# FFN of an MLA layer: the first low-rank input takes the place of one row of the quarter sums, VectorE adds the second one while it evacuates PSUM

## The chip, the core and the metric

The kernel runs on one core of a Trainium2 chip. The metric is the device time of one execution in microseconds (us); of several executions the median is given. The core has a matrix engine (TensorE, PE in the profile, with its weight loads shown as PEld), three engines for elementwise work (VectorE or DVE, ScalarE or ACT, GpSimd or POOL), SyncE (SP), which here only issues transfers, and 16 DMA engines. Each engine carries out its own queue of instructions in order and waits on semaphores for the others.

## The reference

The input x is 8 x 256 x 512, that is 2048 rows of 512. Each row is normalised to xn. An attention part gives s from xn (128 heads, a latent of 64, a rope part of 64), an FFN gives g, and the output is x + s * g. Only the FFN bears on this change. Its weights are quarters that are tiled four times over the inputs, each with a low-rank addition of rank 2:

```python
def _layernorm(x, axis=-1, eps=1e-05):
    m = jnp.mean(x, axis=axis, keepdims=True)
    v = jnp.var(x, axis=axis, keepdims=True)
    return (x - m) / jnp.sqrt(v + eps)
...
    def _qlora_linear(x, wq, A, B):
        w = jnp.tile(wq, (1, 4))
        base = x @ w.T
        lora = x @ A.T @ B.T
        return base + lora * LORA_SCALING
    gate = jax.nn.silu(_qlora_linear(x, w1q, a1, b1))
    up = _qlora_linear(x, w3q, a3, b3)
    return _qlora_linear(gate * up, w2q, a2, b2)
...
x = L0_attn_x
xn = _layernorm(x, axis=-1)
s = _L0_attn_ref(xn, ...)
g = _silu(_L0_ffn_ref(xn, ...))
x = x + s * g
```

w1q and w3q are 1376 x 128, w2q is 512 x 344. Because a weight is tiled four times, x @ w.T is the sum of the four quarters of a row (128 values) times the 128-row quarter weight.

## The kernel before

The program first runs the FFN over all rows (`first_phase`, L304 on), writes the gates to DRAM and then runs the attention, which reads them at its end. The order of the instructions is written out by hand: each engine's queue has the order in which the code issues the instructions, with no scheduler between. All transfers are issued on SP's queue. PSUM has eight banks of 128 x 512 values in float32, one tag for all tiles; a bank comes free when its reader is done. Pools hand out buffers in turn: `f1` has one buffer for a tag, `f2` two.

The rows go in four blocks of 512 (`tb`). The FFN of a block has these parts:

- `norm` (L371 to L403) takes the statistics of the four 128-row tiles on VectorE (L376, L377), and then the reciprocal root in three Newton steps, on VectorE in block 0 and on GpSimd in the others (L393 to L402, 14 small steps). `norm_rest` scales the tiles, on VectorE in block 0 (L412), on ScalarE else (L410).
- `turn` transposes the block on PE (16 transpositions, tile `xpt`, L420); ScalarE copies the even and VectorE the odd results to SBUF (L423, L425). Then the four quarters are added to `xs` (L429 to L431).
- `narrow` computes `pm` on PE (L172), which holds the low-rank inputs of w1 (partitions 0, 1) and w3 (partitions 32, 33), both again at 64 and 96, and the rope keys. VectorE scales it to `mid` (L446). The low-rank inputs are then rows of `mid`. `down` computes `pp` for the attention, and `sum_x` (L157) makes sums of x for the attention, four subtractions on GpSimd.
- The hidden values, 1376, are cut into 11 chunks of 128 columns (the last three hold 88 columns of three quarters, and pieces of the fourth at partitions 96 on). They go in pairs `u` = 0 to 5; the last has one chunk. For each chunk, `low` (L473) starts the banks `px` and `py` with a matmul over the two low-rank rows (two partitions contracted), and `main` adds w1 and w3 times `xs` to them (four matmuls each of 32 output columns and 512 moving ones, L172, called as a `px` or `py` group), evacuates `px` with silu on ScalarE into `gate` (L488, two buffers), and multiplies `gate` with `py` on VectorE (L490, or L493 and L494 for the last three chunks) into `hT`.
- `fold` adds up the hidden quarters on GpSimd (L508 to L510), `low_out` takes their low-rank inputs (four matmuls a third at L520; at the end VectorE adds four parts, L532), and `gate_out` multiplies with w2 (tiles `pf`) and stores the gates.

Between these parts, other work of the attention is put into the queues: `between(0)` calls `set_up` (L598 to L623), which loads `raw`, the mask and others, and rearranges them on GpSimd (L611 on); later calls stand in the last block.

At the start 48 transpositions of the identity (L552) keep PE busy while x is loaded. `load_chunks` fetches the weights in the chunk layout, for w1, w3 and four copies of b13 (the low-rank weights b1 and b3: rows 0, 1 and 32, 33 of a 34-row array). The loop that sets the order of a block is the one at the end of `first_phase`:

```python
            for u in range(6):
                low(tb, u)
                main(tb, u)
                if u in (2, 4):
                    fold(tb, u // 2 - 1)
                    low_out(tb, u // 2 - 1)
                if u == 1 and more:
                    stats = norm(tb + 1)
...
            if more:
                turn(tb + 1)
                low_out(tb, 2)
                narrow(tb + 1)
                down(tb + 1)
```

Of the kernel before, what the change touches and what calls it, by code (L numbers as in the profile page):

```python
# [9 lines left out]
F32 = mybir.dt.float32  # L10
I32 = mybir.dt.int32
AF = mybir.ActivationFunctionType
ALU = mybir.AluOpType
# [24 lines left out]
def mla_ffn_gate_kernel(  # L38
# [42 lines left out]
    cs_d = [dram.tile([P, TB], F32, name=f"cs_d{n}") for n in range(NTB)]  # L81
    krs_d = [dram.tile([R, TB], F32, name=f"kr_d{n}") for n in range(NTB)]
# [221 lines left out]
    def first_phase(between):  # L304
# [8 lines left out]
        b13_sb = fw.tile([98, NCH, P], F32, name="b13_sb")  # L313
# [4 lines left out]
        xts, xns, xnT, xsum, mids = {}, {}, {}, {}, {}  # L318
# [8 lines left out]
        def load_chunks(to, of):  # L327

            of = of.rearrange("p (q f) -> p q f", q=4)
            nc.sync.dma_start(  # L330
                out=to[:, 0:8].rearrange("p (q n) m -> p q (n m)", q=4), in_=of[:, :, 0:256]
            )
            nc.sync.dma_start(out=to[:, 8:11, 0:88], in_=of[:, 0:3, 256:344])
            nc.sync.dma_start(
                out=to[:, 8:10, 96:128],
                in_=of[:, 3, 256:320].rearrange("p (m i) -> p m i", m=2),
            )
            nc.sync.dma_start(out=to[:, 10, 96:120], in_=of[:, 3, 320:344])

        for t in (w1_sb, w3_sb, b13_sb):  # L340
            nc.gpsimd.memset(t[:, 8:11, 88:96], 0.0)
            nc.gpsimd.memset(t[:, 10, 120:128], 0.0)
# [18 lines left out]
        for n in range(2):  # L361
            for k in range(2):
                load_chunks(
                    b13_sb[64 * n + 32 * k : 64 * n + 32 * k + 2], b13[32 * k : 32 * k + 2, :]
                )
        load_chunks(w1_sb, w1t)
        load_chunks(w3_sb, w3t)
        load_x(1)

        def norm(tb):  # L370


            mv = f2.tile([P, 4, 2], F32, tag="mv", name=f"mv_{tb}")
            for n in range(4):
                s6 = f2.tile([P, 6], F32, tag="st", name=f"st_{tb}_{n}")
                nc.vector.bn_stats(s6, xts[tb][n])  # L376
                nc.vector.bn_aggr(mv[:, n, :], s6)  # L377
# [21 lines left out]
            off = f2.tile([P, 4], F32, tag="off", name=f"off_{tb}")  # L399
            if tb:  # L400
                nc.gpsimd.tensor_mul(off, mv[:, :, 0], r)
# [12 lines left out]
        def turn(tb):  # L414
            a = f1.tile([P, KT, TB], F32, tag="act1", name=f"act1_{tb}")
            xnT[tb] = a
            for n in range(4):
# [4 lines left out]
                if n % 2 == 0:  # L422
# [4 lines left out]
            xs = f2.tile([P, TB], F32, tag="xs", name=f"xs_{tb}")  # L427
# [549 lines left out]
```

## Time and profile before

The time before is 2010.74 us, the median of three runs (2010.64 to 2012.42). The profile was taken in an execution of its own:

| quantity | us |
|---|---|
| profiled execution, its own time | 2012.79 |
| its span, from the first to the last instruction of the profile | 2011.0 |
| span before the first transposition of x | 11.2 |
| from there to the first `pm` of block 1 | 42.5 |
| to that of block 2 | 51.5 |
| to that of block 3 | 48.2 |
| the last block of the FFN, with attention work in it | 85.1 |
| the attention | 1772.5 |
| VectorE busy in these four stretches of the FFN | 19.2, 19.5, 19.6, 20.2 |
| ScalarE busy in them | 13.9, 13.6, 14.0, 22.3 |
| GpSimd busy in them | 25.9, 24.4, 21.9, 49.2 |

One median `px` matmul over two low-rank rows (L473) is listed with 0.64 us, one over 128 partitions and 32 output columns (L172) with 0.59; four of the latter run side by side, and matmuls overlap, so that a group's time is read from the distance of starts and not from the sum of durations. Evacuating a bank with silu takes 0.60 (L488), the product on VectorE 0.69 (L490).

How to read the profile: the first part of its page gives each engine's busy time and share of the span. A line of the timeline gives the start, the length, engine, line of the code, operation, what is written and read with its size, and how many were merged; in square brackets the idle time before it and what ended that. The chain that ended last goes back from the last instruction, at each step to what released it or to the instruction before it on its engine. `SPq` is the queue that issues the transfers.

### The profile page before, as it was taken

To read this page: it belongs to the slowest core of one execution; us is meant where nothing else is said; L and a number is where in the kernel's file an instruction comes from. 1 tells how busy PE (TensorE), PEld (TensorE's weight loads), DVE (VectorE), ACT (ScalarE), POOL (GpSimd) and SP (SyncE) were. 2 spreads that over 40 slices of the span, in tenths; PEclk is the share of its full clock that TensorE was granted. 3 is DMA by queue.
4 is the path that set the end of the run, shared out by engine and by line. 5 is a ranking of instruction groups with operands and counts; after the bars stand their busy time and mean duration, and the time that the engine had idled before them with its cause. 6 is when DMAs were issued, how large, how long until landed. Compare 5 with 4: busy or idle time off the path is not lost.

```text
span 2011.0 us, 86602 instructions
## 1 busy us (share of the span) xinstructions
PE 1998.9 (99%) x38112; PEld 1412.7 (70%) x38112; DVE 1522.8 (76%) x2601; ACT 1079.4 (54%) x2958; POOL 725.9 (36%) x1076
## 2 busy tenths in 40 slices
PE   9999999999999999999999999999999999999998
PEld 4334577777777777777777767777777767777776
DVE  4332387878788777878787877878787877888788
ACT  2222365565556554555655645565565555556654
POOL 5445545545552323233233233223323323232231
PEclk9999999999999999999999999999999999999999
DMA  5233322222223223222223233222223222222212
GB/s 169 87 113 135 113 95 84 68 87 86 86 82 123 80 91 112 91 87 78 74 86 123 66 112 105 84 81 86 81 92 102 90 93 81 86 86 72 80 55 70
DMA packets 118188, 184.78 MB, mean 92 GB/s; under 512 B 10450, under 2 KB 84082, under 8 KB 117812
## 3 DMA queue, kind: packets, MB, share of 16 engines
q1 hardware_dynamic: 117812, 179.23, 26.4%
q8 instruction: 302, 4.95, 1.0%
q14 instruction: 74, 0.61, 0.1%
HBM read 145.12 MB, written 34.08 MB: 89 GB/s over the span
## 4 chain that ended last, share of the span: by engine, by line
PE 97%; DVE 2%; issue 0%; DMA 0%; ACT 0%; POOL 0%; SPq 0%; DVEq 0%
PE q L172 39%; PE sc L688 34%; PE av L734 11%; PE po L172 2%; PE pf L172 2%; PE px L172 2%; PE py L172 2%; PE px L473 1%; PE pm L172 1%; PE qq L250 1%; PE vps L285 1%; PE pp L172 1%; DVE pt L717 1%; DVE nmx L701 0%; PE pm L520 0%; PE xpt L420 0%
## 5 line engine op out<-in xcount | busy, mean ns | idle before, releaser
L707 ACT ACTIVATE pr<-sc,nmx 128x256 f32<-128x256 f32 x2048 | 816.5, 502 | 473.8 <-DVE nmx L701 471.0
L701 DVE TENSOR_REDUCE nmx<-sc 128x2 f32<-128x512 f32 x1024 | 635.6, 683 | 291.3 <-PE sc L688 267.4
L717 DVE STREAM_TRANSPOSE pt<-pr 128x512 f32<-128x512 f32 x1024 | 635.2, 678 | 0.0
L172 PE MATMUL q<-x,ws 128*32 128x256 f32 x8192 | 488.9, 379 | 0.6 <-POOL ws L136 0.6
L688 PE MATMUL sc<-act,qr 32*128 32x256 f32 x8192 | 489.0, 374 | 0.0
L215 POOL TENSOR_TENSOR e<-e,e 128x256 f32<-128x256 f32 x128 | 93.8, 733 | 1057.5 <-ACT e L210 570.6
L688 PEld LDWEIGHTS sc<-act,qr 32*128 32x128 f32 x8192 | 421.2, 185 | 22.2 <-issue 0.2
L172 PEld LDWEIGHTS q<-x,ws 128*32 128x32 f32 x8192 | 265.7, 110 | 177.2 <-POOL ws L136 1.1
L172 PE MATMUL q<-x,w 128*32 128x256 f32 x6144 | 381.5, 381 | 0.2 <-DMA w<-in_w_rope_dram 0.2
L172 PEld LDWEIGHTS q<-x,w 128*32 128x32 f32 x6144 | 186.9, 110 | 155.0 <-ACT pr L707 35.4
L688 PE MATMUL sc<-kc,qcm 32*128 32x256 f32 x4096 | 281.2, 387 | 0.0
L734 PE MATMUL av<-pt,vpad 128*32 128x128 f32 x8192 | 236.4, 273 | 1.9 <-ACT pr L707 1.2
L734 PEld LDWEIGHTS av<-pt,vpad 128*32 128x32 f32 x8192 | 226.3, 110 | 14.5 <-issue 3.0
L688 PEld LDWEIGHTS sc<-kc,qcm 32*128 32x128 f32 x4096 | 198.4, 184 | 52.1 <-issue 40.1
L210 ACT COPY e<-q 128x256 f32<-128x256 f32 x512 | 204.1, 399 | 27.9 <-PE q L172 26.3
L754 ACT ACTIVATE acc<-av,sides_sb 128x256 f32<-128x256 f32 (+1 forms) x130 | 54.3, 470 | 245.9 <-PE av L734 245.9
L270 POOL TENSOR_TENSOR qcm<-qc,mask_sb 128x1024 f32<-128x1024 f32 x64 | 122.3, 1911 | 9.6 <-ACT qc L260 9.6
L217 POOL TENSOR_TENSOR qr<-e,e 128x256 f32<-128x256 f32 x128 | 93.7, 732 | 10.0
L216 POOL TENSOR_TENSOR e<-e,e 128x256 f32<-128x256 f32 x128 | 93.5, 731 | 10.0
L227 DVE TENSOR_TENSOR qr<-e,q 128x256 f32<-128x256 f32 x128 | 53.9, 421 | 43.4 <-POOL e L215 24.4
L300 POOL COPY vpad<-vall 32x128 f32<-32x128 f32 x256 | 74.9, 293 | 14.8 <-ACT vall L292 4.4
L490 DVE TENSOR_TENSOR hT<-gate,py 128x512 f32<-128x512 f32 x32 | 21.5, 687 | 73.9 <-PE py L172 47.4
(105 smaller groups left out, 1107.4 us busy)
## 6 DMA issues: line engine op xcount, KB each, us to landing
w<-in_w_rope_dram SPq DMA_DIRECT2D x128, 512.0 KB
ws<-sums_d SPq DMA_DIRECT2D x96, 512.0 KB
sums_d<-ws SPq DMA_DIRECT2D x32, 512.0 KB
x<-xs_d SPq DMA_DIRECT2D x28, 256.0 KB
xt<-in_x_dram SPq DMA_DIRECT2D x16, 256.0 KB
xs_d<-xt SPq DMA_DIRECT2D x16, 256.0 KB
gate_d<-gs SPq DMA_DIRECT2D x16, 256.0 KB
g<-gate_d SPq DMA_DIRECT2D x16, 256.0 KB
```

The costliest lines, as they stand in the source:

```text
L172: nc.tensor.matmul(to[tile_], w[:, tile_], x, start=start, stop=stop, skip_group_check=True)
L210: nc.scalar.copy(self.e[i], self.banks[i])
L215: nc.gpsimd.tensor_add(m6, m6, m1)
L216: nc.gpsimd.tensor_add(m7, m7, m6)
L217: nc.gpsimd.tensor_add(self.out(1, 1), self.split(m7), self.split(m5))
L270: nc.gpsimd.tensor_mul(qcm, qks[b, sg // 2][0].rearrange("p (q i) -> p q i", i=32).unsqueeze(2).to_broadcast([P, 8, 4, 32]), mask_sb[:, ds ...
L300: nc.gpsimd.tensor_copy(vpad[rows, :, :, 8 * t + 4 * (sg % 2) :][..., :4], valls[b][rows, :, sg])
L688: nc.tensor.matmul(sc[r][:, h, :], lhs.rearrange("p t i -> p (t i)"), rhs, start=(part == 0 and h == 0), stop=(part == 2), skip_group_chec ...
L701: nc.vector.tensor_reduce(nmx[:, r, :], scs[n, f][r], AX.X, ALU.max, negate=True)
L707: nc.scalar.activation(p[:, h, :], scs[n, f][r][:, h, :], AF.Exp, bias=nmxs[n, f][:, r, h : h + 1])
L717: nc.vector.transpose(pts[n, f // 2, r].rearrange("p k q i -> p q k i")[:, ds(2 * (f % 2), 2)], prs.pop((n, f, r)).rearrange("p h (k j) -> ...
L734: nc.tensor.matmul(av[32 * r : 32 * r + 32, ds(half * P, P)], vpad[:, k, r, :], pt[r][:, k].rearrange("p q i -> p (q i)"), start=(k == 0), ...
```

## The change

Each row of xn adds up to zero over its 512 values. So the 128 quarter sums of a row add up to zero too, and quarter sum 0 is minus the sum of the others. The change subtracts row 0 of w1 and w3 from all their rows; the product with the quarter sums stays the same, and row 0 of the weights becomes zero and row 0 of the sums free. Into these free rows go the first low-rank weight (row 0 or 32 of b13) and the first low-rank input (row 0 or 32 of `mid`), in two copies of the sums, one for w1 and one for w3 (`xs0`, `xs1`). The second low-rank input is sent to DRAM (`low_d`) and back to all partitions (`low0`, `low1`); VectorE multiplies it with the second low-rank weight, a value for each partition (`bcol_sb`), and adds the bank of `px` or `py`, in one instruction that evacuates the bank. The matmuls of `low` are gone. ScalarE's silu then runs in place in SBUF, and the product of a pair's first chunk (of the first eight chunks) goes to GpSimd.

To prepare this, row 0 of w1 and w3 and all of b13 are loaded as plain rows (`rows`) by ScalarE's queue, which also loads b13's rows into row 0 of the weights; PE spreads row 0 of the weights over the partitions (`first`), turns the second low-rank weights into columns (`bcol`), and ScalarE copies them out of PSUM; GpSimd subtracts (`less_first`). The rest of w1 and w3, rows 1 to 127, comes through SP's queue in five pieces each in place of four. The warm-up at the start is 16 and 8 transpositions. The statistics of the next block are spread over the pairs 0 to 3, the copies in `turn` are all on ScalarE from block 1 on, and `narrow` is moved ahead of the last `low_out`.

```diff
+    low_d = [dram.tile([2, TB], F32, name=f"low_d{n}") for n in range(NTB)]
...
-        b13_sb = fw.tile([98, NCH, P], F32, name="b13_sb")
+        bcol_sb = fw.tile([P, 2, NCH], F32, name="bcol_sb")
...
-        xts, xns, xnT, xsum, mids = {}, {}, {}, {}, {}
+        xts, xns, xnT, xsum, lows = {}, {}, {}, {}, {}
         def load_x(tb):
...
-        def load_chunks(to, of):
+        def by_chunks(to, of):
...
-            nc.sync.dma_start(
-                out=to[:, 0:8].rearrange("p (q n) m -> p q (n m)", q=4), in_=of[:, :, 0:256]
-            )
-            nc.sync.dma_start(out=to[:, 8:11, 0:88], in_=of[:, 0:3, 256:344])
-            nc.sync.dma_start(
-                out=to[:, 8:10, 96:128],
-                in_=of[:, 3, 256:320].rearrange("p (m i) -> p m i", m=2),
-            )
-            nc.sync.dma_start(out=to[:, 10, 96:120], in_=of[:, 3, 320:344])
-        for t in (w1_sb, w3_sb, b13_sb):
+            for q in (0, 2):
+                yield (
+                    to[:, 2 * q : 2 * q + 4].rearrange("p (q n) m -> p q (n m)", q=2),
+                    of[:, q : q + 2, 0:256],
+                )
+            yield to[:, 8:11, 0:88], of[:, 0:3, 256:344]
+            yield to[:, 8:10, 96:128], of[:, 3, 256:320].rearrange("p (m i) -> p m i", m=2)
+            yield to[:, 10:11, 96:120], of[:, 3:4, 320:344]
+        def load_chunks(engine, to, of):
+            for one, two in by_chunks(to, of):
+                engine.dma_start(out=one, in_=two)
+        rows = f1.tile([P, 3 * TB], F32, tag="h4", name="rows")[:, 0:F]
+        nc.scalar.dma_start(out=rows[64:65], in_=w1t[0:1, :])
+        nc.scalar.dma_start(out=rows[96:97], in_=w3t[0:1, :])
+        nc.scalar.dma_start(out=rows[0:34], in_=b13)
+        others = f2.tile([P, TB], F32, tag="gate", name="others")[:, 0:P]
+        nc.gpsimd.memset(others, 1.0)
+        nc.gpsimd.memset(others[:, 0:1], 0.0)
+        nc.gpsimd.memset(bcol_sb, 0.0)
+        for t in (w1_sb, w3_sb):
...
-        for n in range(2):
-            for k in range(2):
-                load_chunks(
-                    b13_sb[64 * n + 32 * k : 64 * n + 32 * k + 2], b13[32 * k : 32 * k + 2, :]
-                )
-        load_chunks(w1_sb, w1t)
-        load_chunks(w3_sb, w3t)
+        for k, (w_sb, wt) in enumerate(((w1_sb, w1t), (w3_sb, w3t))):
+            load_chunks(nc.scalar, w_sb[0:1], b13[32 * k : 32 * k + 1, :])
+            load_chunks(nc.sync, w_sb[1:128], wt[1:128, :])
...
+        mvs = {}
+        def norm_part(tb, n):
+            if n == 0:
+                mvs[tb] = f2.tile([P, 4, 2], F32, tag="mv", name=f"mv_{tb}")
+            s6 = f2.tile([P, 6], F32, tag="st", name=f"st_{tb}_{n}")
+            nc.vector.bn_stats(s6, xts[tb][n])
+            nc.vector.bn_aggr(mvs[tb][:, n, :], s6)
         def norm(tb):
-            mv = f2.tile([P, 4, 2], F32, tag="mv", name=f"mv_{tb}")
-            for n in range(4):
-                s6 = f2.tile([P, 6], F32, tag="st", name=f"st_{tb}_{n}")
-                nc.vector.bn_stats(s6, xts[tb][n])
-                nc.vector.bn_aggr(mv[:, n, :], s6)
+            mv = mvs[tb]
...
-            off = f2.tile([P, 4], F32, tag="off", name=f"off_{tb}")
+            off = None
...
+                off = f2.tile([P, 4], F32, tag="off", name=f"off_{tb}")
...
-                if n % 2 == 0:
+                if tb or n % 2 == 0:
...
-            xs = f2.tile([P, TB], F32, tag="xs", name=f"xs_{tb}")
+            xs = [f1.tile([P, TB], F32, tag=f"xs{k}", name=f"xs{k}_{tb}") for k in range(2)]
...
-            nc.vector.tensor_add(xs, a[:, 0, :], a[:, 1, :])
+            nc.vector.tensor_add(xs[0], a[:, 0, :], a[:, 1, :])
...
-            nc.vector.tensor_add(xs, xs, xs2)
+            nc.vector.tensor_add(xs[0], xs[0], xs2)
+            nc.scalar.copy(xs[1], xs[0])
...
         def over_xn(tb, name, weights):
...
-            mids[tb] = mid
+            nc.sync.dma_start(out=low_d[tb], in_=mid[1:34:32, :])
+            lows[tb] = []
+            for k in range(2):
+                t = f1.tile([P, TB], F32, tag=f"low{k}", name=f"low{k}_{tb}")
+                nc.sync.dma_start(out=t, in_=low_d[tb][k : k + 1, :].to_broadcast([P, TB]))
+                lows[tb].append(t)
+                nc.scalar.copy(xsum[tb][k][0:1], mid[32 * k : 32 * k + 1])
...
-        sets, hTs, h4s, mid2ps = {}, {}, {}, {}
+        hTs, h4s, mid2ps = {}, {}, {}
         def pair(u):
...
-        def low(tb, u):
-            sets[tb, u] = []
-            for i, c in enumerate(pair(u)):
-                for k in range(2):
-                    ps = bank(f"p{'xy'[k]}_{tb}_{u}_{i}")
-                    r = slice(64 * i + 32 * k, 64 * i + 32 * k + 2)
-                    nc.tensor.matmul(
-                        ps, b13_sb[r, c], mids[tb][r], start=True, stop=False, skip_group_check=True
-                    )
-                    sets[tb, u].append(ps)
         def main(tb, u):
...
-            for i, c in enumerate(pair(u)):
-                px, py = sets[tb, u][2 * i : 2 * i + 2]
-                on_columns(px, w1_sb[:, c], xsum[tb], False, True)
-                on_columns(py, w3_sb[:, c], xsum[tb], False, True)
-                gate = f2.tile([P, TB], F32, tag="gate", name=f"gate_{tb}_{u}_{i}")
-                nc.scalar.activation(gate, px, AF.Silu)
-                if c < 8:
-                    nc.vector.tensor_mul(h[:, c // 2, :], gate, py)
-                else:
+            chunks = pair(u)
+            gates, ups = [], []
+            for i, c in enumerate(chunks):
+                px, py = (bank(f"p{'xy'[k]}_{tb}_{u}_{i}") for k in range(2))
+                on_columns(px, w1_sb[:, c], xsum[tb][0], True, True)
+                on_columns(py, w3_sb[:, c], xsum[tb][1], True, True)
+                gates.append(f2.tile([P, TB], F32, tag="gate", name=f"gate_{tb}_{u}_{i}"))
+                ups.append((py, h[:, c // 2, :] if i == 0 and u < 5 and c < 8 else py))
+                nc.vector.scalar_tensor_tensor(
+                    gates[i], lows[tb][0], bcol_sb[:, 0, c : c + 1], px, ALU.mult, ALU.add
+                )
+                nc.scalar.activation(gates[i], gates[i], AF.Silu)
+                nc.vector.scalar_tensor_tensor(
+                    ups[i][1], lows[tb][1], bcol_sb[:, 1, c : c + 1], py, ALU.mult, ALU.add
+                )
+            for c, gate, (py, up) in zip(chunks, gates, ups):
+                if c >= 8:
...
+                elif up is py:
+                    nc.vector.tensor_mul(h[:, c // 2, :], gate, py)
+                else:
+                    nc.gpsimd.tensor_mul(up, gate, up)
         def fold(tb, n):
...
-        idle = bank("idle")
-        for n in range(48):
-            nc.tensor.transpose(idle[:, ds(n % 4 * P, P)], ident, ident)
+        def warm(count):
+            idle = bank(f"idle{count}")
+            for n in range(count):
+                nc.tensor.transpose(idle[:, ds(n % 4 * P, P)], ident, ident)
+        warm(16)
+        firsts = []
+        spots = [(slice(0, 3), slice(0, 88)), (slice(0, 2), slice(96, 128)), (slice(2, 3), slice(96, 120))]
+        for k in range(2):
+            to = f2.tile([P, 4, TB], F32, tag="hT", name=f"first_{k}")
+            to = to.rearrange("p a m -> p (a m)")[:, 0 : NCH * P].rearrange("p (c m) -> p c m", m=P)
+            of = slice(64 + 32 * k, 65 + 32 * k)
+            for i, (one, two) in enumerate(by_chunks(to, rows[of])):
+                if i < 2:
+                    ps = bank(f"first_{k}_{i}").rearrange("p (q m) -> p q m", q=2)
+                else:
+                    if i == 2:
+                        third = bank(f"first_{k}_2")[:, 0 : 3 * P]
+                        third = third.rearrange("p (c m) -> p c m", m=P)
+                    ps = third[:, spots[i - 2][0], spots[i - 2][1]]
+                nc.tensor.matmul(
+                    ps, others[of], two, start=True, stop=True, skip_group_check=True
+                )
+                nc.scalar.copy(one, ps)
+            firsts.append(to)
+        for k in range(2):
+            ps = bank(f"bcol{k}")
+            r = slice(32 * k, 32 * k + 2)
+            second = ident[r, 32 * k + 1 : 32 * k + 2]
+            for c in range(NCH):
+                q, n = (c // 2, c % 2) if c < 8 else (c - 8, 2)
+                one = rows[r, ds(q * FQ + n * P, CH[n][1])]
+                nc.tensor.matmul(ps[0 : CH[n][1], c : c + 1], one, second, start=True, stop=True)
+                if c >= 8:
+                    m = 32 if c < 10 else 24
+                    one = rows[r, ds(3 * FQ + 256 + 32 * (c - 8), m)]
+                    nc.tensor.matmul(
+                        ps[96 : 96 + m, c : c + 1], one, second, start=True, stop=True
+                    )
+            for p_, c_ in (
+                (slice(0, P), slice(0, 8)),
+                (slice(0, 88), slice(8, 11)),
+                (slice(96, 128), slice(8, 10)),
+                (slice(96, 120), slice(10, 11)),
+            ):
+                nc.scalar.copy(bcol_sb[p_, k, c_], ps[p_, c_])
+        warm(8)
+        def less_first(k):
+            w_sb = (w1_sb, w3_sb)[k]
+            for one, two in (
+                (w_sb[:, 0:8], firsts[k][:, 0:8]),
+                *((w_sb[:, 8:11][:, a, b], firsts[k][:, 8:11][:, a, b]) for a, b in spots),
+            ):
+                nc.gpsimd.tensor_sub(one, one, two)
+        for n in range(4):
+            norm_part(0, n)
...
+        less_first(0)
...
+        less_first(1)
...
             for u in range(6):
-                low(tb, u)
...
-                if u == 1 and more:
+                if u < 4 and more:
+                    norm_part(tb + 1, u)
+                if u == 3 and more:
...
             if more:
...
+                narrow(tb + 1)
...
-                narrow(tb + 1)
```

## The prediction

> **What bounds the kernel now.** First the page: TensorE (PE) is busy for the whole span, and the chain that ended last is 97% PE.
>
> ```profile
> span 2011.0 us, 86602 instructions
> ...
> PE 1998.9 (99%) x38112; PEld 1412.7 (70%) x38112; DVE 1522.8 (76%) x2601; ACT 1079.4 (54%) x2958; POOL 725.9 (36%) x1076
> ...
> PE 97%; DVE 2%; issue 0%; DMA 0%; ACT 0%; POOL 0%; SPq 0%; DVEq 0%
> ```
>
> The change touches only the FFN, the first 238 us. Next the chain in order of time (start, length, work):
>
> ```profile
> 11.17 3.61 PE xpt L420 x16
> 14.78 3.59 PE pm L172 x64
> 18.37 3.43 PE pp L172 x32
> ...
> 53.69 3.64 PE pm L172 x32
> ...
> 122.55 0.62 PE px L473
> ...
> 153.39 3.64 PE pm L172 x32
> ```
>
> PE starts on x at 11.17, and the blocks follow. Call that start X. Third, PE's timeline in block 0, one pair of chunks to the next:
>
> ```profile
> 36.70 0.69 PE L473 MATMUL px<-mid,b_sb 2*128 2x512 f32 x1
> ...
> 37.77 1.07 PE L172 MATMUL px<-xs,w_sb 128*32 128x512 f32 x8
> ...
> 41.34 0.69 PE L473 MATMUL px<-mid,b_sb 2*128 2x512 f32 x1
> ```
>
> A pair lasts 41.34 - 36.70 = 4.64 us. Its four groups at L172 are 0.86 each on the chain, 3.43.
>
> **Low-rank matmuls removed: up to -28.9.** 4.64 - 3.43 = 1.21 for the four matmuls of a pair; the sixth, half pair costs the same 1.2 (46.84 to 49.76 less two groups of 0.86). Six times 1.2 is 7.2 a block, 28.9 over four, if PE stays the bound. The subtracted row itself costs PE nothing.
>
> **Work for VectorE: it replaces PE as the bound in blocks 0 to 2.**
>
> ```profile
> 61.18 2.14 DVE L532 SCALAR_TENSOR_TENSOR h<-pm,h 32x512 f32<-32x512 f32 x3
> ...
> 77.69 1.29 DVE L490 TENSOR_TENSOR hT<-gate,py 128x512 f32<-128x512 f32 x2 [13.58 <-ACT gate L488]
> ```
>
> The added instruction is L532's, also reading PSUM: 0.71 in a dependent row of three, 0.65 where neighbours are independent as at L490. I take 0.65, since neighbours here belong to different banks. A pair has four and one product, 3.25, and one statistics part of 0.8 (L376 with L377): 4.05 against PE's 3.43. Eight PSUM banks hold PE's lead to two pairs. So in a middle block, from its first px: 1.1 to the first eviction, four pairs 16.2 and three small operations 0.6 (17.9); the 14 GpSimd steps of the norm 3.9 (41.51 to 45.39 in block 0); four scalings 2.9 (L410); last transposition and copies about 3: pm at 27.9. Then pm 3.6, the moved low_out 1.0, pp 3.4, pf 10.3: 46.2 us. GpSimd's products (1.3, as L508) fit between its folds. Before, block 1 took 122.5 - 71.0 = 51.5 (with a stall for gate transfers, which the longer head now covers) and block 2 170.8 - 122.5 = 48.3: -5.3 and -2.1. At 0.71 the two gains shrink by 3 together. In the last block PE also has attention work between pairs, VectorE has slack, and I count -6.5 of 7.2, the rest lost to GpSimd, whose products queue behind sum_w.
>
> **Block 0: +11.** GpSimd's products stand in its queue behind set_up and the four subtractions of sum_x.
>
> ```profile
> 27.48 0.41 POOL L611 COPY wup_sb<-raw 128x64 f32<-128x64 f32 x2 [9.57 <-DMA raw<-in_w_up_dram]
> ...
> 40.27 1.27 POOL L157 TENSOR_TENSOR xt<-act,xt 128x512 f32<-128x512 f32 x1
> 41.51 0.20 POOL L393 TENSOR_TENSOR e<-r 128x4 f32<-128x4 f32 x1
> ```
>
> They end at 41.55, X+30.4, and still will: the raw transfer stays behind mid in SP's queue; low_d and its two broadcasts, now ahead of it, cost some 3 us, about what emptier queues give back. The first product ends at X+31.7. The gate tile has two buffers, and the built program makes the fourth eviction (gate_1_1) wait for that product; all of VectorE's later evictions are queued behind it, and PE's banks with them. From there 2.8 + 8.1 + 0.6 to the last statistics (X+43.2), 3.9, 2.9 and 2.7 to pm: X+52.7, against 53.69 - 11.17 = X+42.5 before. With low_out moved behind pm: +11.
>
> Blocks together: 11 - 5.3 - 2.1 - 6.5 = -2.9, bounds -9 (set-up lands early) to +4 (0.71 everywhere).
>
> **Start-up: +80, the largest term.** Between the warm-up and the first transposition PE now does ten matmuls (first) and 28 tiny ones (bcol), and ScalarE evacuates them. ScalarE first issues 13 transfers, then loads its table, all in order. The w1 and w3 loads cover rows 1 to 127. How many DMA engines serve them? Packet counts in four stretches tell what row counts did before:
>
> ```profile
> DMA packets 10, 0.01 MB, mean 27 GB/s; under 512 B 2, under 2 KB 10, under 8 KB 10
> ...
> DMA packets 429, 0.73 MB, mean 81 GB/s; under 512 B 86, under 2 KB 86, under 8 KB 427
> ...
> q1 hardware_dynamic: 427, 0.70, 24.0%
> ...
> DMA packets 288, 0.52 MB, mean 150 GB/s; under 512 B 32, under 2 KB 32, under 8 KB 288
> ...
> q1 hardware_dynamic: 1161, 0.54, 102.4%
> ```
>
> Here data packets have 1 or 2 KB, so the small ones are end marks. Around 10.4 us: a 2-row b13 load, 8 packets and 2 marks. At 252 to 261: 4-row wo loads, 341 data packets, 16 to a load, so 21.3 loads and 86 marks, 4 each. At 236.5 to 240: two 128-row stores, 32 marks, 16 each. I read one mark as one engine: the count used divides the rows, up to 16. The trace has no 127-row transfer; bounds are 16 engines, as for 128 rows, and one, the only divisor of 127. "As many as rows, up to 16" fits the rows too. I take one, since no transfer here used a count that leaves a remainder, and keep 16 as a rival. That all ten loads use the same engine isn't shown either; the packets carry no engine number. I assume it, because a fixed first engine is the simplest rule, and keep different engines in the same rival.
>
> The Trainium skill, DMA: Bandwidth & Descriptors, section Why a DMA increments its semaphore by 16 and not by 1, says that the count is the largest number up to 16 that divides the slowest dimension of both sides, names 127 partitions as one engine, and puts such transfers on the lowest-numbered engine. By it the sum is the one-engine case below; by 16 engines it is the rival's 2026; no run here shows it yet.
>
> Price of one engine: 24.0% of 16 engines over 9 us for 0.70 MB is 49 us a MB (wo, 2 KB packets); 102.4% over 2 us for 0.54 MB is 61 (15 to 17 us, the same w loads on full queues). 2 x 127 x 1376 x 4 B = 1.398 MB: 69 to 85 us, I take 77, from about 8 us, when x, kr and a have gone.
>
> Each transfer takes one of eight completion counters, and its issue waits until the counter's last user has landed; SP shows such waits already:
>
> ```profile
> SPq L338 <- DMA xt<-in_x_dram: 0.6, 1, 0.6
> ```
>
> ScalarE's last but one transfer shares its counter with the second big w3 piece. That piece ends 13% (0.18 of 1.4 MB) before the whole: 8 + 67 = 75. Two issues of 0.45 (as SP's) and the table load of 1.28 (L423): 77. Then five copies for w1 2.8 (0.59 each for 512 columns, 0.4 for 264, 0.2 small, with PE's turns), w3's matmuls and copies 3.7, bcol's 56 passes 6.5 (0.11 each, a 32-column weight load; bounds 3.4 at q's 0.054 spacing and 10.2 at 0.182), eight transpositions 1.2: X = 91. Bounds: 8 + 60 + 2.2 + 11 = 81 and 8 + 74 + 2.2 + 18 = 102. Against 11.17: +80 (70 to 91). Queued behind it are all transpositions, hence pm, mid, set_up and every block. GpSimd's weight subtractions (some 4 us each, from L508's 1.3 for 512 columns) lie under these waits or under pm and pp.
>
> The clock already sags here: 9 to 13 us was granted 0.77 and 13.6 to 15 us 0.65.
>
> The Trainium skill, TensorE: Matmul & The Clock Gate, section What's actually happening, gives half clock after an idle window of about 3.4 us and as long to recover; by it the transpositions and pm would lose at most 1.7 us more, by the rows about nothing, as they start slow already; I add nothing.
>
> **Sum.** 80 - 2.9 = +77 on the profiled execution (span 2011.0, its own time 2012.79, 2.05 above the median of 2010.74). Outside the FFN nothing changes. 2010.7 + 77 = 2088; its own range 2072 (70 - 9) to 2106 (91 + 4).
>
> **Rivals.**
> - The loads use 16 engines, or a different one each. For: 128 rows did use 16. Against: the divisors. With 16 the issues wait for pieces landing at 9.5, 12 and 12.9; ScalarE is free at 15, and 14 us of work make X = 29 (24 to 33), +18 - 2.9: 2026. With one engine each, the largest piece (127 x 512 x 4 B, 0.26 MB) takes 16 at most, lands at 24, and X is 40: 2037. Together 2016 to 2040. Chance 0.11.
> - Faster. One mechanism, in the start-up: the w1 and w3 pieces don't hold the preparation up, ScalarE's copies run while x is still loaded and normalised, and GpSimd's set_up, which follows its transfer, keeps its old time after X, so that block 0 stays as it was. Price: X at 13 (+2), blocks -5.3 - 2.1 - 6.5 = -13.9, together -12: 1999. For: ScalarE is nearly idle before 11, and 24 transpositions fewer are left in the warm-up. Against: the 13 issues at 0.45 and the table load alone end at 7.1, with 14 us of copies and bcol behind them. It decides if X stays under about 21 (11.2 + 13.9 less the 4 us of a real gain) with block 0 unchanged; with block 0's +11, X would have to stay under 10. Chance 0.06.
> - In between, blocks and start-up cancelling (X at 14, block 0 +11: +2.8 - 2.9): 2011. Chance 0.02.
>
> **Numbers.** Forecast 0.81. With its tails the range is 2055 to 2115, which holds nearly all of it and leaves out 2 in 10. 0.2% (4 us) is what a measurement can tell from no change. Faster 0.06, same 0.02, slower 0.92.
>
> **What will show it.** Right: after's first xpt near 91; first copies (line 601) near 77; the engines at about 6% share (one of 16) from 10 to 85 us; no px from a mid; DVE waiting for GpSimd once in block 0; blocks 1 and 2 near 46. Wrong: share near 100% until 13 us, then X near 29 (16 engines); PE passing X before 14; block 0 with no wait for a product.

## The result, and the profile after

The changed kernel takes 2097.93 us (median of four, 2096.72 to 2099.05) beside 2011.29 of the kernel before: a ratio of 1.043, 95% interval 1.0412 to 1.0448. It is 86.6 us slower; 2088 was forecast. The first lines of its page, to be held against those shown of before:

```profile
span 2097.2 us, 86533 instructions
...
PE 1997.3 (95%) x37988; PEld 1441.4 (69%) x37988; DVE 1570.3 (75%) x2667; ACT 1094.2 (52%) x2994; POOL 754.2 (36%) x1101
...
PE 89%; DVE 3%; SPq 3%; DMA 2%; POOL 1%; ACT 1%; issue 1%; ACTq 0%; POOLq 0%; DVEq 0%
```

PE's busy time hardly fell (1998.9 to 1997.3), its share fell from 99% to 95%: the time lies between its instructions. The stages, each from one start on PE's timeline to the next, beside the forecast and two later versions, c1_all and c2_order, which are described with the experiments:

| stage, us | before | forecast | after | c1_all | c2_order |
|---|---|---|---|---|---|
| to the first transposition of x | 11.2 | 91 | 93.0 | 11.2 | 10.1 |
| block 0, to `pm` of block 1 | 42.5 | 53.5 | 55.1 | 45.6 | 38.5 |
| block 1 | 51.5 | 46.2 | 49.8 | 54.3 | 44.0 |
| block 2 | 48.2 | 46.2 | 48.2 | 45.4 | 41.5 |
| block 3, to the end of its `pf` | 85.1 | 78.6 | 79.9 | 81.8 | 78.9 |

The forecast of block 0 is the +11, which counts 1.0 for the `low_out` moved behind `pm`; up to `pm` itself it was 52.7. The start-up gave +81.8, the blocks +5.7; what follows the FFN took 1771.3 where it had taken 1772.5. Together that is 86.3, the difference of the spans (86.2) but for rounding. Why the start-up takes so long is seen on two queues. SyncE's timeline (start, length of the issue, what is loaded, how many):

```profile
5.42 38.34 SPq L343 DMA_DIRECT2D w_sb<-in_w1t_dram  x5
43.80 35.06 SPq L343 DMA_DIRECT2D w_sb<-in_w3t_dram  x5
```

ScalarE's timeline, the same columns:

```profile
3.58 67.55 ACTq L343 DMA_DIRECT2D w_sb<-in_b_dram  x10
71.16 1.28 ACT L601 ACT_TABLE_LOAD   x1 [71.16 <-DMA w_sb<-in_b_dram]
```

And the transfer view of 10 to 70 us:

```profile
DMA packets 1951, 1.28 MB, mean 21 GB/s; under 512 B 865, under 2 KB 1951, under 8 KB 1951
...
q1 hardware_dynamic: 1921, 1.27, 7.1%
```

The queue's packets took 7.1% of sixteen engines' time, hardly more than one engine's 6.25%, at 21 GB/s. SyncE could not even issue: five loads took 38 us, five more 35. ScalarE, with ten little row loads between, got to its table at 71.16. Nothing else happens: PE, VectorE and GpSimd show no instruction between 15 and 70 us. After that the preparation is on the path, as the chain of waits has it (start, length, work):

```profile
44.99 25.05 DMA w_sb<-in_w3t_dram
...
81.56 3.28 PE bcol L610 x16
86.16 3.79 PE bcol L610 x18
...
93.16 2.57 PE xpt L439 x16
```

In the blocks, VectorE's timeline shows the wait for GpSimd in block 0 and the length of a pair in block 1, from the first eviction of one pair to the next (174.99 to 179.23, 4.24 us):

```profile
126.08 0.75 DVE L507 SCALAR_TENSOR_TENSOR gate<-low,bcol_sb,px 128x512 f32<-128x512 f32 x1 [8.21 <-POOL hT L524]
...
174.99 0.73 DVE L507 SCALAR_TENSOR_TENSOR gate<-low,bcol_sb,px 128x512 f32<-128x512 f32 x1
...
179.23 0.73 DVE L507 SCALAR_TENSOR_TENSOR gate<-low,bcol_sb,px 128x512 f32<-128x512 f32 x1
```

PE's timeline shows the end of blocks 0 and 1:

```profile
148.07 5.92 PE L173 MATMUL pm<-act,ck_sb 128*32 128x512 f32 x32 [0.88 <-ACT act L442]
...
193.28 3.53 PE L439 MATMUL xpt<-ident,xt 128*128 128x128 f32 x16 [3.34 <-ACT xt L429]
197.83 3.64 PE L173 MATMUL pm<-act,ck_sb 128*32 128x512 f32 x32 [1.02 <-ACT act L442]
```

The kernel before had at the same two places:

```profile
53.69 3.64 PE L172 MATMUL pm<-act,ck_sb 128*32 128x512 f32 x32 [0.37 <-DVE act L425]
...
102.09 1.97 PE L420 MATMUL xpt<-ident,xt 128*128 128x128 f32 x16
...
105.17 3.64 PE L172 MATMUL pm<-act,ck_sb 128*32 128x512 f32 x32
```

PE, whose one wait there had been 0.37, waits 3.34 for the scaling of x and 1.02 for the last copy; and one `pm` took 5.92 where its like took 3.64.

### The profile page after: what moved, and what is told of

Its sections match the earlier page's. It is cut to its first block, busy times and chain, and to the rows that moved or that the text cites. A ratio compares the mean times of both kernels' runs of the same rounds, so it can differ in the third digit from the quotient of the medians.

```text
span 2097.2 us, 86533 instructions
## 1 busy us (share of the span) xinstructions
PE 1997.3 (95%) x37988; PEld 1441.4 (69%) x37988; DVE 1570.3 (75%) x2667; ACT 1094.2 (52%) x2994; POOL 754.2 (36%) x1101
## 3 DMA queue, kind: packets, MB, share of 16 engines
q8 instruction: 301, 4.93, 1.0%
## 4 chain that ended last, share of the span: by engine, by line
PE 89%; DVE 3%; SPq 3%; DMA 2%; POOL 1%; ACT 1%; issue 1%; ACTq 0%; POOLq 0%; DVEq 0%
PE q L173 38%; PE sc L774 32%; PE av L820 10%; PE po L173 2%; SPq L343 2%; PE pf L173 1%; DMA w_sb<-in_w3t_dram 1%; PE qq L251 1%; PE vps L286 1%; DVE gate L507 1%; PE px L173 1%; DVE pt L803 1%; PE py L173 1%; PE pm L173 0%; DVE nmx L787 0%
## 5 line engine op out<-in xcount | busy, mean ns | idle before, releaser
L173 PE MATMUL q<-x,ws 128*32 128x256 f32 x8192 | 495.0, 379 | 0.1
L173 PEld LDWEIGHTS q<-x,ws 128*32 128x32 f32 x8192 | 273.1, 110 | 171.0 <-POOL ws L137 0.6
L173 PE MATMUL q<-x,w 128*32 128x256 f32 x6144 | 387.6, 381 | 0.0
L173 PEld LDWEIGHTS q<-x,w 128*32 128x32 f32 x6144 | 192.8, 110 | 150.1 <-ACT pr L793 35.8
L211 ACT COPY e<-q 128x256 f32<-128x256 f32 x512 | 203.7, 399 | 20.5 <-PE q L173 17.8
L840 ACT ACTIVATE acc<-av,sides_sb 128x256 f32<-128x256 f32 (+1 forms) x130 | 54.3, 470 | 246.5 <-PE av L820 246.5
L301 POOL COPY vpad<-vall 32x128 f32<-32x128 f32 x256 | 75.3, 294 | 10.6 <-PE av L820 2.7
L598 PE MATMUL first<-rows,others 1*128 1x512 f32 (+3 forms) x20 | 11.3, 734 | 65.3 <-ACT first L601 65.3
```

The costliest lines, as they stand in the source:

```text
L173: nc.tensor.matmul(to[tile_], w[:, tile_], x, start=start, stop=stop, skip_group_check=True)
L211: nc.scalar.copy(self.e[i], self.banks[i])
L301: nc.gpsimd.tensor_copy(vpad[rows, :, :, 8 * t + 4 * (sg % 2) :][..., :4], valls[b][rows, :, sg])
```

## The experiments

**e1_112_15.** The loads of rows 1 to 127 are cut into 112 and 15 rows:

```diff
-            load_chunks(nc.sync, w_sb[1:128], wt[1:128, :])
+            load_chunks(nc.sync, w_sb[16:128], wt[16:128, :])
+            load_chunks(nc.sync, w_sb[1:16], wt[1:16, :])
```

> The changed kernel with each w1 and w3 load cut into rows 16 to 127 (112 rows) and rows 1 to 15 (15 rows); same bytes, same queue, twice the pieces. If the count of engines that serve a 127-row load is the cause (mine): the pieces land by about 15 us, the first transposition of x starts at 29 (25 to 34) in place of 93.2, and the time is 2034 (2028 to 2040). If instead ScalarE's thirteen issues, the completion counters or the number of pieces hold the start-up up, with more pieces now: the first transposition stays beyond 60 and the time beyond 2065.

Measured: 2046.22 (ratio to the kernel before 1.0177, interval 1.016 to 1.0194), 51.7 less than the changed kernel with the same bytes on the same queue in twice the pieces. PE's timeline:

```profile
27.91 3.63 PE L611 MATMUL bcol<-ident,rows 2*128 2x1 f32 x17
...
39.65 3.39 PE L440 MATMUL xpt<-ident,xt 128*128 128x128 f32 x16
```

The view by stretches has, for 15 to 20 us (stretch, length, busy time of PE, PEld, DVE, ACT and POOL, then the granted clock, DMA share and GB/s), as the loads of w3 follow those of w1:

```profile
15.00:20.00 5.00, 0.00 (x0) 0.00 (x0) 0.00 (x0) 2.13 (x3) 0.00 (x0) 0.50 0.52 122
```

That is 122 GB/s in place of 21. The count of engines is the cause, and the rival is out. But the first transposition came at 39.65 and not at 29. ScalarE's table load began at 17.86, and from its end, 19.14, the preparation took 20.5 us, where I had reckoned with 14. The forecast has the same hole; it is taken up below.

**b1_127.** The reverse, in the kernel before: only the loads of w1 and w3 cut into row 0 and rows 1 to 127.

```diff
-        load_chunks(w1_sb, w1t)
-        load_chunks(w3_sb, w3t)
+        for w_sb, wt in ((w1_sb, w1t), (w3_sb, w3t)):
+            load_chunks(w_sb[0:1], wt[0:1, :])
+            load_chunks(w_sb[1:128], wt[1:128, :])
```

> The kernel before with only its w1 and w3 loads cut into row 0 and rows 1 to 127. If one engine serves 127 rows: the first transposition stays at 11.2, the first group on w3 starts near 75 (70 to 85) in place of 22.7, the DMA engines show about 7% of 16 engines until then, and the time is 2060 (2052 to 2068), some 50 more, since a part of block 0's waiting for the mask at 29.8 is covered. If 127 rows go over 16 engines: 2011 (2009 to 2013).

Measured: 2079.74 (1.0342, interval 1.0326 to 1.0357), 69 more than before from the loads of two arrays. SyncE's timeline, and after it PE's:

```profile
15.01 0.68 SPq L330 DMA_DIRECT2D w_sb<-in_w1t_dram  x1
15.74 19.18 SPq L333 DMA_DIRECT2D w_sb<-in_w1t_dram  x1
```

```profile
78.77 1.94 PE L172 MATMUL py<-xs,w_sb 128*32 128x512 f32 x8 [36.00 <-DMA w_sb<-in_w3t_dram]
```

The mechanism and the place are as expected (first transposition 11.24, first w3 group at 78.8, 7% of the engines), the sum was 20 too small and the time outside its range: I had counted on block 0's wait for the mask being covered, but the mask's load stands behind the slow ones in SyncE's queue, and PE waited another 9.3 us at 98.4.

**e2_dve0.** In block 0 all products on VectorE:

```diff
-                ups.append((py, h[:, c // 2, :] if i == 0 and u < 5 and c < 8 else py))
+                ups.append((py, h[:, c // 2, :] if tb and i == 0 and u < 5 and c < 8 else py))
```

> The changed kernel with all products of block 0 on VectorE instead of half of them on GpSimd. If the wait of VectorE for GpSimd's first product (8.2 us, GpSimd still at set_up and the sums) is what lengthens block 0: that wait is gone, four products of 0.65 come back, so 5.6 less (3 to 8): 2092 (2090 to 2095). If VectorE's own work or the late low-rank broadcast sets block 0: no change or slower, 2097 to 2101.

Measured: 2093.46 (2091.53 to 2094.94), 4.5 less than the changed kernel's 2097.93, in the range. VectorE no longer waits for GpSimd in block 0, and in the profiled runs, which lie 7.0 apart, the block fell from 55.1 to 48.3. It is still 5.8 longer than before. VectorE's timeline shows what comes next:

```profile
112.60 0.16 DVE L703 TENSOR_REDUCE sides_sb<-mask_sb 128x2 f32<-128x8 f32 x1 [10.86 <-DMA mask_sb<-in_kmask_dram]
```

The sum over the mask stands ahead of the first eviction in VectorE's queue. From there VectorE works without a gap to the block's last pairs, so this wait and VectorE's own work set the block once GpSimd's is gone; c1_all and c2_order move the sum to block 2.

**h1_up_only.** The kernel before with the trick for w3 alone. Core of the edit:

```diff
-                for k in range(2):
-                    ps = bank(f"p{'xy'[k]}_{tb}_{u}_{i}")
-                    r = slice(64 * i + 32 * k, 64 * i + 32 * k + 2)
-                    nc.tensor.matmul(
-                        ps, b13_sb[r, c], mids[tb][r], start=True, stop=False, skip_group_check=True
-                    )
+                px, py = (bank(f"p{'xy'[k]}_{tb}_{u}_{i}") for k in range(2))
+                r = slice(64 * i, 64 * i + 2)
+                nc.tensor.matmul(
+                    px, b1_sb[r, c], mids[tb][r], start=True, stop=False, skip_group_check=True
+                )
...
-                on_columns(py, w3_sb[:, c], xsum[tb], False, True)
+                on_columns(py, w3_sb[:, c], xsum[tb][1], True, True)
+                nc.vector.scalar_tensor_tensor(
+                    py, lows[tb], bcol_sb[:, c : c + 1], py, ALU.mult, ALU.add
+                )
```

> The kernel before with the trick for w3 alone: py loses its low-rank matmul (44 instead of 88), w3 in 112 and 15 rows, px keeps its matmul and goes to ScalarE as before, all products on VectorE, no change to the order of the statistics, and the sum over the mask moved out of block 0's VectorE queue. Theory: the trick itself pays where PE stays the bound; 44 matmuls of 0.30 are 13 less, the mask's wait some 3 to 6 less, start-up the same (11 to 13): 1994 (1987 to 2001). Rival: the preparation (five copies of ScalarE, GpSimd's subtraction of 4 us after w3 has landed, the broadcast through DRAM) holds block 0 up by as much as the matmuls give: 2003 to 2012. Second rival: VectorE's eleven added instructions a block (0.65 each) become the bound: slower than 2011.

Measured: 2017.98 (1.0036, interval 1.0023 to 1.0049), a miss. The start-up took 4.6 more (first transposition at 15.8). Block 0 took 45.2, 2.7 more; blocks 1 and 2 took 50.6 and 48.9, where they had taken 51.5 and 48.2, and PE's timeline in block 2 says why they gained nothing (two pairs):

```profile
133.57 1.13 PE L485 MATMUL px<-mid,b_sb 2*128 2x512 f32 x4
...
138.20 1.13 PE L485 MATMUL px<-mid,b_sb 2*128 2x512 f32 x4
```

From pair to pair it is 4.63, as with all four matmuls (4.64), and PE has no wait in these pairs, so VectorE (the second rival) is not what bounds them. The kernel before shows them on PE's timeline as follows:

```profile
122.48 0.69 PE L473 MATMUL px<-mid,b_sb 2*128 2x512 f32 x1
122.48 0.69 PE L473 MATMUL py<-mid,b_sb 2*128 2x512 f32 x1
122.49 0.69 PE L473 MATMUL px<-mid,b_sb 2*128 2x512 f32 x1
122.50 0.69 PE L473 MATMUL py<-mid,b_sb 2*128 2x512 f32 x1
```

All four start within 0.02 us: each uses another strip of 32 partitions, and they run side by side. My 0.30 for one of them was a quarter of a group that has only one price, 1.2 for two or for four; the prediction had read that off the half pair, whose two cost the same 1.2. The Trainium skill, TensorEngine Tiling (Array Packing), section Key Properties, says that tiles of the array work independently; these rows, 0.02 us apart, agree.

**e3_gs4 and e4_stats_head** ask why blocks 1 and 2 gained less than forecast. The first gives the gates four buffers on their way to DRAM (`gs` with `bufs=3`, its third tile in `h4b`, `mid` with one buffer), the second moves the statistics of the next block:

```diff
+            if more:
+                for n in range(4):
+                    norm_part(tb + 1, n)
+                stats = norm(tb + 1)
             for u in range(6):
...
-                if u < 4 and more:
-                    norm_part(tb + 1, u)
-                if u == 3 and more:
-                    stats = norm(tb + 1)
```

> The changed kernel with four buffers for the gates on their way to DRAM in place of two (mid gives up one of its two). In blocks 1 and 2 ScalarE waits 3.6 and about 4 us for the store of the first gate tile before it takes the third, and the first silu of the pairs stand behind it. If that wait is what keeps the two blocks from the forecast gain (mine): both get 3 shorter (2 to 4.5), 2092 (2089 to 2095). If VectorE's own work sets these blocks and catches up later: 2096 to 2099.

> The changed kernel with the statistics of the next block and its norm ahead of the six pairs instead of one part in each of four pairs, while PE is at pm, pp and pf. If VectorE is the bound in the pairs: a pair falls from 4.24 to about 3.45, and PE's wait for the scaling before the transpositions (3.4 us) goes: blocks 1 and 2 get 3 to 6.5 shorter each, 2088 (2083 to 2093). If the gate stores or GpSimd's products set the blocks: less than 2 in all, 2096 to 2099.

Measured: 2097.82 (2097.17 to 2099.34) for e3_gs4 and 2096.53 (2091.07 to 2100.53) for e4_stats_head, beside 2097.93. Both missed. In e3_gs4 ScalarE's wait of 3.6 for the stores is gone, but the first pair of block 1 is only 0.5 shorter, 4.9 instead of 5.5 from its first eviction to the next pair's, because VectorE was evicting in the meantime. In its profiled run the start-up and block 0 were 0.8 and 1.6 longer; the cause is open. At the end of block 2 PE all the same reached the next `pm` 1.7 earlier than in the changed kernel (244.27 for 246.01) and lost it there, on PE's timeline:

```profile
244.27 5.36 PE L173 MATMUL pm<-act,ck_sb 128*32 128x512 f32 x32 [1.17 <-ACT act L442]
```

In e4_stats_head blocks 1 and 2 shrank by 2.0 and 1.5 from `pf` to `pf`, and block 0 grew by 4.4; there VectorE waited 9.5 for GpSimd, whose late products now had the 14 norm steps ahead of them. PE's wait for the scaling is gone, but one for the last copy takes its place, and the next `pm` is long, here at the end of block 1:

```profile
198.92 5.34 PE L173 MATMUL pm<-act,ck_sb 128*32 128x512 f32 x32 [2.62 <-ACT act L442]
```

Neither edit by itself frees the blocks.

**c1_all and c2_order** put the findings together. c1_all prepares on the host, by copying alone, what the start-up had computed or loaded in pieces, and keeps e3_gs4 and e4_stats_head. It also moves set_up to block 1 and the sum over the mask to block 2:

```diff
+            nc.sync.dma_start(out=w_sb.rearrange("p c m -> p (c m)"), in_=wc)
...
+            nc.sync.dma_start(out=to, in_=firstc[k : k + 1, :].to_broadcast([P, NCH * P]))
...
+        nc.sync.dma_start(out=bcol_sb.rearrange("p k c -> p (k c)"), in_=bcol)
...
-        less_first(0)
         turn(0)
-        less_first(1)
+        less_first()
         narrow(0)
-        between(0)
...
+            if tb == 1:
+                between(0)
```

> The change with all that was found: w1 and w3 laid out on the host in chunks with the first low-rank row in row 0 (one load of 128 rows each), the subtracted row broadcast by a load, the low-rank columns loaded as columns (no matmul and no copy before the transpositions), GpSimd's subtraction after the first transpositions, set_up moved from block 0 to the head of block 1, the sum over the mask to block 2, statistics ahead of the pairs, four gate-store buffers. Theory: first transposition at 11 to 13 (80 less), block 0 40 to 44 (12 less), blocks 1 and 2 41 to 45 (5 to 9 less each): 1992 (1984 to 2001), faster than before. Rival: GpSimd, with the subtractions, set_up, products and folds, or VectorE at the end of a block sets the blocks: 2003 to 2015.

Measured: 2012.35 (1.0008, interval 0.9998 to 1.0017): the start-up is back at 11.2, and with it the time, but the four blocks together take 227.1, as in the kernel before (227.3): the rival's case. VectorE's timeline shows where in blocks 0 and 1, PE's at the end of block 2:

```profile
18.38 7.45 DVE L427 TENSOR_TENSOR xs<-xs,xs 128x512 f32<-128x512 f32 x1 [2.96 <-POOL xs L426]
...
92.08 0.75 DVE L484 SCALAR_TENSOR_TENSOR gate<-low,bcol_sb,px 128x512 f32<-128x512 f32 x1 [8.77 <-POOL hT L501]
```

```profile
156.50 6.61 PE L174 MATMUL pm<-act,ck_sb 128*32 128x512 f32 x32 [2.62 <-ACT act L419]
```

An addition of VectorE lasts 7.45 beside GpSimd's subtractions (18.31 to 25.17); set_up in block 1 holds a product up just as it had in block 0; and at a block's end ScalarE's copies of `xpt` stand behind the silu of the last half pair, which stands behind VectorE's backlog. c2_order therefore changes the order:

```diff
+                if u == 5 and more:
+                    turn(tb + 1)
                 main(tb, u)
...
-                if u == 4 and more:
+                if u == 3 and more:
                     norm_rest(tb + 1, *stats)
...
             if more:
-                turn(tb + 1)
+                add_up(tb + 1)
                 narrow(tb + 1)
-                low_out(tb, 2)
                 down(tb + 1)
-            else:
-                low_out(tb, 2)
+            low_out(tb, 2)
```

where `add_up` is the second half of `turn`; in block 0 GpSimd does its addition. set_up's loads are issued in block 0, its GpSimd work follows the sums of block 1, block 0's first two pairs have all products on VectorE, and the statistics for block 1 stand ahead of block 0's third pair.

> The kernel before this one (c1_all) with another order: the transpositions of the next block ahead of the last half pair, its scaling after pair 3, GpSimd adds the sums of block 0 before it subtracts (VectorE's add took 7.45 us beside it), the products of block 0's first two pairs on VectorE, set_up's loads in block 0 and its GpSimd work ahead of the norm in block 1, the last low_out after pp. Theory: what kept blocks 1 to 3 from the gain of the removed matmuls is the end of a block (ScalarE's copies queued behind the last silu, PE idle for 2.6 and then at half clock: pm 5.3 to 6.6 in place of 3.64) and set_up ahead of a product; block 0 41 to 46 (from 45.6, first transposition to pm), block 1 41 to 46 (from 54.3), block 2 40 to 43 (from 45.4): 1994 (1986 to 2002). Rival: VectorE, with 30 us of work in a block of 41, and GpSimd stay the bound in the pairs: 2003 to 2011.

Measured: 1989.61 (0.9891, interval 0.9875 to 0.9908): 20.7 faster than the kernel before, 108 than the changed one. PE's timeline:

```profile
48.62 3.64 PE L174 MATMUL pm<-act,ck_sb 128*32 128x512 f32 x32
...
92.61 3.64 PE L174 MATMUL pm<-act,ck_sb 128*32 128x512 f32 x32
...
134.10 3.62 PE L174 MATMUL pm<-act,ck_sb 128*32 128x512 f32 x32
```

There is no wait ahead of `pm`, and each takes its 3.6. The edits of c2_order were not tried apart. The table's rows add up to 25.5 less than before; what follows the FFN took 2.4 more (1774.9), and the profiled execution of the kernel before was itself 2.4 above the median of these runs.

**b3_order** gives the kernel before, with its low-rank matmuls, the same order where it applies (the edit just shown, copies of `turn` on ScalarE, the statistics behind the first pair from block 1 on, the sum over the mask in block 2).

> The kernel before, with its low-rank matmuls, in c2_order's order where that applies: transpositions of the next block ahead of the last half pair and their copies on ScalarE, scaling after pair 3, statistics ahead of the pairs from block 1 on, the last low_out after pp, the sum over the mask in block 2. If c2_order's 21 come from matmuls that are gone, and the order only lets the gain through: PE had 0.6 us of idle time after its first transposition of x, so 2010 (2007 to 2012). If the order itself is the gain: below 2000.

Measured: 2007.9 (0.9989, interval 0.9979 to 0.9999). The order alone is worth some 2.5 us. In the four blocks PE was busy for 222.7 of 224.2 us here and for 196.4 of 202.8 in c2_order (226.7 of 227.3 in the kernel before). So what b3_order lacks beside the missing matmuls, the gate buffers and the place of set_up, could free little more than the 1.5 us that PE stood idle. The rest of c2_order's 20.7 comes with the matmuls that are gone and with the start-up's new loads, whose share is at most the 1.1 of the table's first row.

## Why the prediction was right, step by step

**One engine for 127 rows: right, and shown from both sides** by e1_112_15 and b1_127. It was inferred from counts of end marks (2, 4 and 16 for 2, 4 and 128 rows); the choice of "the count divides the rows" over "as many as rows, up to 16" carried the forecast. The Trainium skill's rule in DMA: Bandwidth & Descriptors, section Why a DMA increments its semaphore by 16 and not by 1, said the same, also that such transfers share the lowest-numbered engine; 7.1% and 21 GB/s over ten loads agree with one shared engine, and no row here gives its number.

**The start-up, 91 forecast and 93.0 measured, is right by two errors that cancel, which is luck.** The end of the table load was put at 77 and came at 72.4: the loads ran a little faster than the fast end of the price (1.27 MB in 60 us is 47 us a MB, where 49 to 61 was taken). The counter that ScalarE's last issues wait for was read rightly: the chain has them follow the w3 piece that landed at 70.04. From there to the first transposition 14.2 was forecast and 20.5 measured (20.7 on the chain, which begins it at 93.16). The undersized terms are the copies and matmuls of `first` (9.1 against 6.5, since the two engines wait for each other at each piece), `bcol`, 9.7 against 6.5, and the eight transpositions, 1.9 against 1.2. The clock is not among them: it was granted as 1.00 here and as 0.50 in e1_112_15, and the same work took 20.5 in both. `bcol` was priced by the 0.11 us of a 32-column weight load; 44 of the 56 passes load 88 or 128 columns, so the nearest row was the 128-column one at 0.182, which stood in the text as the upper bound (10.2).

**Low-rank matmuls: right in sum.** All four of a pair are gone and a pair on PE is 3.43 in block 3. The four as one group were priced rightly; the price of one by itself, used in h1_up_only, was not.

**VectorE as the new bound: right in kind, 5.6 too small in blocks 1 and 2** (46.2 each against 49.8 and 48.2). A pair is 4.24 instead of 4.05, since a product has to wait for the eviction just ahead of it (0.86 from start to start in place of 0.65): 0.8 over four pairs. The first pair is 1.2 and 1.9 longer than the others; e3_gs4, where it took 4.93 in both blocks, puts 0.5 and 1.25 of that down to the gate stores, which the prediction had taken for covered. In block 1, `pm` took 2.3 longer, which no step had foreseen. These come to 7.0 over both blocks; the other parts of the two blocks were 1.4 shorter than forecast.

**Block 0: right, and 2.4 too small.** Up to `pm` 52.7 was forecast and 55.1 measured, with the wait for GpSimd's first product at the fourth eviction; e2_dve0 removed it. That product ended 33.1 after the first transposition in place of 31.7, and VectorE's pairs behind it took 1.1 longer. **Block 3** gained 5.2 of the 6.5 forecast. So the blocks' sum, -2.9 with bounds -9 and +4, came out at +5.7, outside its bounds; the start-up was inside its own, and their sum, 86.6 against 77, inside the forecast's range.

**The rivals.** "Faster" named its condition, the preparation done before x is normalised. c1_all met its part on the start-up (11.2) but not the one that block 0 stays as it was (45.6 for 42.5), and gained nothing; its block 1 took 54.3, where 46.2 was reckoned. It took the order of c2_order as well. Its price, 1999, lies between the two. The rival with 16 engines fell with e1_112_15, whose 2046 also shows two holes in its 2026: the first transposition came 10.6 later than its 29, and the rest lies in the blocks, which its sum took over from the forecast.

## What to carry to other kernels

Before cutting a row off a load, look at what the rows divide into: one row less of 128, in two arrays, cost some 70 us here, and the issuing queue was held up with it, so that whatever stands behind pays too. An instruction that runs beside its like has no price of its own: divide a group's time among its members only when starts on the timeline lie apart. When a bound is taken off one engine, follow the end of each stage through every queue before counting the gain: here the same removed matmuls were worth nothing in c1_all and most of 21 us in c2_order, by the order of the instructions and the engine of a few of them.

## What was not expected of the hardware

**Waits that cost twice.** PE idled for 2.6 to 4.5 us around the transpositions, and its next `pm` then took 5.9 (the changed kernel), 5.4 (e3_gs4) or 6.6 (c1_all, after the 2.62) instead of 3.64, but not always. The view by stretches of the changed kernel (stretch, length, busy time of PE, PEld, DVE, ACT and POOL, then the granted clock, DMA share and GB/s) for the `pm` of blocks 1 and 2:

```profile
148.00:154.00 6.00, 5.93 (x36) 1.53 (x40) 2.22 (x2) 0.02 (x1) 5.84 (x6) 0.61 0.01 3
...
197.80:201.50 3.70, 3.67 (x36) 1.20 (x40) 0.87 (x1) 0.00 (x0) 3.62 (x4) 1.00 0.02 4
```

The clock was 0.61 in the one and 1.00 in the other, after nearly the same idle times (3.50 and 0.88; 3.34 and 1.02). Whether a short wait costs the clock can't be told from its length here: 2.62 in c1_all did (0.50 from 156.5 to 160.5), 4.36 in the changed kernel did not.

**An issue that blocks.** In b1_127 the first load of 127 rows was issued in 0.68 us, like one of 128 rows (about 0.6); the issue of the next one behind it kept SyncE for 19.18.

**VectorE held up by GpSimd.** The addition of two SBUF tiles took 0.69 alone in the kernel before and 7.45 in c1_all, where GpSimd subtracted from 18.31 to 25.17 and it ended 0.66 later. In the changed kernel it took 2.86 and ended before GpSimd's four subtractions did (101.28 and 102.37), so that it is not always held to the last of them.
